# Experts' output rows: two sums by the token's choice, additions without an order, sums read on two queues

## The chip, the core and the metric

The kernel runs on one core of a Trainium2 chip. Its engines are TensorE (PE, matrix products, with PEld for the loading of weights), VectorE (DVE), ScalarE (ACT), GpSimd (POOL) and SyncE (SP). Each works through its own queue of instructions in order; an instruction waits until the semaphores that it names have their values, and everything behind it on that queue waits too. DMAs are issued on SP's, ACT's and POOL's queues and run on 16 DMA engines. The metric is the time of the program on the device in microseconds (us); lower is better.

## What is computed

Four layers over 4096 tokens of 128 numbers: an attention (a, causal), a layer of experts, a second attention (b), and the same layer of experts again, each on the normalised input and added to its input. The layer of experts is what the change is about:

```python
x = x + _L0_attn_a_ref(_layernorm(x, axis=-1), ...)
x = x + _L0_ffn_ref(_layernorm(x, axis=-1), Wr, Wg, Wu, Wd)
x = x + _L0_attn_b_ref(_layernorm(x, axis=-1), ...)
x = x + _L0_ffn_ref(_layernorm(x, axis=-1), Wr, Wg, Wu, Wd)

# _L0_ffn_ref: 8 experts, each token goes to its best two
logits = flat_x @ Wr
top_vals, top_idx = jax.lax.top_k(logits, 2)
rw = jax.nn.softmax(top_vals, axis=-1)
combine = jnp.sum(rw[..., None] * jax.nn.one_hot(top_idx, 8), axis=1)
g = jnp.einsum('nc,ech->neh', flat_x, Wg)      # 128 -> 512
u = jnp.einsum('nc,ech->neh', flat_x, Wu)
h = jax.nn.silu(g) * u
eo = jnp.einsum('neh,ehc->nec', h, Wd) / sqrt(12)
out = jnp.einsum('ne,nec->nc', combine, eo)
```

## The kernel before

**Stages.** `attention` works on 8 blocks (`NB`) of 512 tokens. Its instructions are written out in a fixed order for every engine (the `InOrder` wrappers `te`, `ve`, `se`, `po`, `sy`), by a small planner of tasks with due rounds. At the end of a block, `finish` adds the attention's output to `x`, stores the 512 rows to DRAM (L846) and calls `route`. `route` picks for each token its two experts and writes two copies of its normalised row, one for each choice, to the list of that expert's rows in `rows_in`: 128 numbers, the token's number, and its weight. `both_rows` holds the two copies (index 0 the first choice, 1 the second); the token's number is put in by one copy on GpSimd (L342), from `tokens`, the same number for both.

**Experts.** `experts` then takes the lists in 39 tiles (`TILES`) of 256 rows (`TE`), two halves of 128 (`ET` = 2). For each tile `fetch` loads on SyncE's queue the row block `x_in` (six buffers) and the weights of its expert, `w_g`, `w_u`, `w_d`; `turned` transposes the rows (`xT`); TensorE computes `pg` and `pu`, ScalarE `sg` = silu(`pg`), VectorE `h` = `pu` x `sg`, TensorE `py` from `h` and `w_d`. `finish` of experts multiplies `py` by the rows' weights into `y` (L1015), and for each half of the tile GpSimd issues an indirect DMA that adds 128 rows of `y` to rows of a sum in DRAM (L1019, `compute_op=ALU.add`), at the token numbers in `to`. Outside `attention`, the order of an engine's instructions is chosen when the program is built; program order is only a priority there.

**Where the rows go.** `places` makes `to` in three instructions on VectorE: `here` = 1 for rows of the tile that are filled (L1004), `here` x (token - `nobody`) (L1005), plus `nobody` (L1009). A row that is not filled goes to row 4096 + its partition, which nobody reads. `here` has two buffers, `to` six, `y` four.

**The sums.** For each layer of experts there are two sums, `totals[i][0]` and `totals[i][1]`, DRAM tiles of 4224 rows. The first is filled by the attention's stores (L846), the second with zeros (`zeros`, steps that the first attention spreads over its rounds); the first half of each tile is added to the first, the second half to the second (`sums[(i * ET + s) % 2]`). Since a token's two rows can be added to the same sum, additions to one sum are ordered: each waits until the one before it into the same sum has landed.

**Reading.** The second attention loads a block as `xb` from the first sum and `more` from the second, both on SyncE's queue (L528, L532; `more` has one buffer), and adds them on GpSimd (L541). After the last layer, SyncE's queue loads `a` and `b` for each of 8 blocks, VectorE adds them (L1074) and SyncE's queue stores the result (L1071 to L1075). `tokens_of` gives a partition four rows that lie 128 rows apart, so a DMA moves pieces of one row, 512 bytes.

Instructions issued through an `InOrder` wrapper all show L222 in the profile, whatever line called them; there the names of the tiles tell them apart.

Of the kernel before, what the change touches and what calls it, by code (L numbers as in the profile page):

```python
# [33 lines left out]
F32 = mybir.dt.float32  # L34
# [4 lines left out]
ALU = mybir.AluOpType  # L39
# [3 lines left out]
P = 128  # L43
# [8 lines left out]
NE = 8  # L52
HID = 512
NC = HID // P
TB = 512
NT = TB // P
# [4 lines left out]
ET = TE // P  # L61
CAP = 17 * TE
TOKENS = 4096
W = P + 2
# [6 lines left out]
def layers(  # L71
# [21 lines left out]
    nc = tc.nc  # L93
    xt = x.flatten_outer_dims().rearrange("(n t p) d -> n p t d", t=NT, p=P)
    ot = out.flatten_outer_dims().rearrange("(n t p) d -> n p t d", t=NT, p=P)
    NB = xt.shape[0]
# [17 lines left out]
    def attention_weights(wq, bq, wk, bk, wv, bv, wo, bo, scale, name):  # L114
# [45 lines left out]
    half = const.tile([P, NE], F32, name="half")  # L160
# [14 lines left out]
    tokens = const.tile([P, NB * NT], F32, name="tokens")  # L175
    within = tokens[:, 0:ET]
    nobody = const.tile([P, 1], F32, name="nobody")
# [4 lines left out]
    totals = [  # L182
        [dram.tile([TOKENS + P, P], F32, name=f"total{i}{j}") for j in range(2)] for i in range(2)
    ]
    blank = const.tile([P, 3 * W], F32, name="blank")
    wr_sb = const.tile([P, NE], F32, name="wr_sb")

    def zeros():
# [5 lines left out]
        for first, second in totals:  # L194
            flat = second.rearrange("(p a m) d -> p a (m d)", p=P, m=3)
            for k, m in ((0, 4), (4, 8), (8, 11)):
                to = flat[:, k:m, :]
                yield sy.dma_start(
                    out=to,
                    in_=blank[:, 0 : 3 * P].unsqueeze(1).to_broadcast([P, to.shape[1], 3 * P]),  # L200
                )
            yield sy.dma_start(out=first[TOKENS : TOKENS + P, :], in_=blank[:, 0:P])

# [35 lines left out]
    def later_constants():  # L239
# [19 lines left out]
        for t, pattern, base, by_partition in (  # L259
# [4 lines left out]
            (tokens, [[P, NB * NT]], 0, 1),  # L264
            (nobody, [[0, 1]], TOKENS, 1),
        ):
# [65 lines left out]
    def route(pool, psum, n, xb, free, sent):  # L332
# [11 lines left out]
            tokens[:, n * NT : (n + 1) * NT].unsqueeze(1).to_broadcast([P, 2, NT]),  # L344
# [135 lines left out]
    def tokens_of(total, n):  # L480
        return total[n * TB : (n + 1) * TB, :].rearrange("(t p) d -> p t d", p=P)
# [27 lines left out]
    def attention(w, causal, name):  # L509
        with ExitStack() as own:  # L510
# [11 lines left out]
            def loaded(n):  # L522
# [110 lines left out]
            def scales(n, q, k, junk):  # L633
# [38 lines left out]
                po.tensor_tensor(den, den, half[:, 0:2], ALU.pow)  # L672
# [160 lines left out]
            def finish(n, o):  # L833
# [12 lines left out]
                sy.dma_start(out=tokens_of(totals[0 if causal else 1][0], n), in_=xs[n])  # L846
# [106 lines left out]
    def experts(name, tiles, sums, last):  # L953
        with ExitStack() as own:
# [5 lines left out]
            table, left, sent = tiles  # L960

            def fetch(i):
# [38 lines left out]
            def places(i, x_in):  # L1001

                here = pool.tile([P, ET], F32, tag="here")
                nc.vector.tensor_scalar(here, within, left[:, i : i + 1], None, ALU.is_lt)  # L1004
                nc.vector.scalar_tensor_tensor(  # L1005
                    here, x_in[:, :, P], nobody, here, ALU.subtract, ALU.mult
                )
                to = pool.tile([P, ET], I32, tag="to", bufs=6)
                nc.vector.tensor_scalar(to, here, nobody, None, ALU.add)  # L1009
                return to  # L1010

            def finish(py, i, x_in):
# [5 lines left out]
                for s in range(ET):  # L1018
                    nc.gpsimd.indirect_dma_start(  # L1019
                        out=sums[(i * ET + s) % 2],  # L1020
                        out_offset=bass.IndirectOffsetOnAxis(ap=to[:, s : s + 1], axis=0),
                        in_=y[:, s, :], in_offset=None, compute_op=ALU.add,
                    )

# [91 lines left out]
```

## Time and profile before

| | us |
|---|---|
| three runs | 1331.39, 1349.69, 1356.59 |
| their median | 1349.69 |
| the profiled execution | 1343.86 |
| its span, first to last instruction | 1342.2 |
| stage A, `y` of the first tile to `y` of the 38th | 434.98 to 644.40 |
| second attention's first read of `more` issued | 655.38 |
| stage B, the same | 1098.69 to 1307.54 |
| last addition issued, last store issued | 1314.19, 1338.91 |

The granted TensorE clock was 0.872 of full speed over the span and 1.00 in both stages of experts. Times in the profile are counted from the first instruction. A line of the timeline gives the start, the length, the engine (with q for its sequencer, which issues DMAs), the line, the operation, the tile written and the tiles read, their shape, and in brackets how long the engine was idle before it and what ended that. A wait for several things is put down to the one that came last.

### The profile page before, as it was taken

The page shows a single profiled execution, that of the slowest core. Times are in us where ns is not written, and L with a number is a line of the kernel's source. Part 1 is how long each engine was busy: PE and PEld are TensorE (multiplying, and loading weights), DVE is VectorE, ACT ScalarE, POOL GpSimd, SP SyncE. Part 2 cuts the span into 40 slices and gives each one's busy share as a digit, 9 for nine tenths or more (in the row PEclk, how much of TensorE's full clock was granted, in tenths as well). Part 3 has the DMA queues.
Part 4 walks back from the last instruction along what each step waited for, and adds up shares of the span by engine and source line. Part 5 has one row for each costly group of instructions (what it writes and reads, how often), then busy time and mean ns, then how long its engine had stood idle before and what let it go on. Part 6 is the DMA issues. An engine that isn't in the chain of part 4 may idle for free. (4 is left out here: it accounts for less than half of the span.)

```text
span 1342.2 us, 23350 instructions
## 1 busy us (share of the span) xinstructions
PE 1066.8 (79%) x8116; PEld 771.8 (58%) x8116; DVE 787.6 (59%) x2221; ACT 518.8 (39%) x942; POOL 594.0 (44%) x599
## 2 busy tenths in 40 slices
PE   2799888898763999999457888778877459999990
PEld 1455555555543888888324454445554248888880
DVE  3667667776533555454258787888675535554541
ACT  1156445554521222222135756665555212222220
POOL 7444546655552555555330114233323325555551
PEclk9889878888855999999757999998788779999995
DMA  4244324530015877776253324133300087777757
GB/s 98 51 97 109 72 73 117 138 84 24 25 36 169 210 188 189 180 195 133 45 109 81 66 58 104 51 78 83 89 23 30 27 230 192 178 187 189 189 103 195
DMA packets 175301, 150.84 MB, mean 112 GB/s; under 512 B 14286, under 2 KB 136784, under 8 KB 175184
## 3 DMA queue, kind: packets, MB, share of 16 engines
q1 hardware_dynamic: 145310, 127.18, 34.8%
q0 software_dynamic: 26560, 18.76, 9.4%
q10 hardware_dynamic: 3314, 3.41, 1.1%
q8 instruction: 65, 1.06, 0.3%
q14 instruction: 52, 0.43, 0.1%
HBM read 82.74 MB, written 31.75 MB: 85 GB/s over the span
## 5 line engine op out<-in xcount | busy, mean ns | idle before, releaser
L1019 POOL DMA_INDIRECT total<-y,to x156 | 242.8, 1556 | 229.2 <-DVE here L1005 59.3
L222 DVE TENSOR_REDUCE mx<-s 128x6 f32<-128x768 f32 (+1 forms) x256 | 277.1, 1084 | 110.4 <-PE s L222 109.4
L222 ACT ACTIVATE p<-s 128x768 f32<-128x768 f32 (+1 forms) x256 | 232.9, 916 | 192.2 <-PE s L222 170.2
L1061 ACT ACTIVATE sg<-pg 128x256 f32<-128x256 f32 x312 | 119.4, 383 | 316.8 <-PE pg L1049 300.7
L1063 DVE TENSOR_TENSOR h<-pu,sg 128x256 f32<-128x256 f32 x312 | 131.9, 423 | 149.6 <-PE pu L1053 147.2
L222 POOL DMA_INDIRECT rows_in<-both_rows,slots x128 | 128.9, 1007 | 172.2 <-DVE both_rows L222 113.0
L1053 PE MATMUL pu<-xT,w_u 128*128 128x256 f32 x624 | 190.2, 387 | 5.7 <-DVE h L1063 5.5
L1049 PE MATMUL pg<-xT,w_g 128*128 128x256 f32 x624 | 192.6, 391 | 1.2 <-DMA w_g<-in_L_ffn_Wg_dram 0.7
L1028 PEld LDWEIGHTS py<-w_d,h 128*128 128x128 f32 x1248 | 163.8, 192 | 8.1
L1028 PE MATMUL py<-w_d,h 128*128 128x128 f32 x1248 | 164.6, 275 | 0.0
L222 PE MATMUL s<-k,q 62*128 62x256 f32 (+1 forms) x1024 | 144.3, 367 | 16.1 <-DMA k<-lo 11.4
L222 PE MATMUL s<-q,k 64*128 64x256 f32 (+1 forms) x1024 | 114.2, 307 | 42.1 <-DVE mx L222 33.5
L222 PE MATMUL av<-p,v 128*32 128x256 f32 (+1 forms) x2048 | 144.5, 406 | 0.3 <-ACT au L222 0.2
L222 PEld LDWEIGHTS s<-k,q 62*128 62x128 f32 x1024 | 89.2, 216 | 87.7 <-issue 51.8
L1053 PEld LDWEIGHTS pu<-xT,w_u 128*128 128x128 f32 x624 | 118.0, 192 | 29.6 <-DVE h L1063 13.8
L222 POOL TENSOR_SCALAR_AFFINE_SELECT p<-p 128x512 f32<-128x512 f32 x128 | 82.5, 645 | 108.3 <-ACT p L222 103.7
L222 PEld LDWEIGHTS s<-q,k 64*128 64x128 f32 x1024 | 89.5, 213 | 58.9 <-DVE mx L222 39.7
L1049 PEld LDWEIGHTS pg<-xT,w_g 128*128 128x128 f32 x624 | 102.2, 194 | 20.3 <-issue 13.8
L222 PEld LDWEIGHTS av<-p,v 128*32 128x32 f32 x2048 | 58.7, 120 | 55.2 <-issue 26.4
L222 POOL TENSOR_TENSOR lo<-to,hi 128x512 fp32r<-128x512 f32 x24 | 30.6, 1273 | 72.4 <-ACT hi L222 72.3
L996 PE MATMUL ps<-ident,x_in 128*128 128x128 f32 x156 | 30.6, 279 | 39.1 <-DMA x_in<-rows_in 39.1
L222 PE MATMUL s<-mask_q,ident_h 128*128 128x256 bf16 x256 | 58.6, 317 | 0.0
(206 smaller groups left out, 1179.3 us busy)
## 6 DMA issues: line engine op xcount, KB each, us to landing
w_g<-in_L_ffn_Wg_dram SPq DMA_DIRECT2D x78, 256.0 KB
w_u<-in_L_ffn_Wu_dram SPq DMA_DIRECT2D x78, 256.0 KB
w_d<-in_L_ffn_Wd_dram SPq DMA_DIRECT2D x78, 256.0 KB
x_in<-rows_in SPq DMA_DIRECT2D x78, 130.0 KB
k<-hi SPq DMA_DIRECT2D x32, 256.0 KB
k<-lo SPq DMA_DIRECT2D x32, 256.0 KB
q<-hi SPq DMA_DIRECT2D x28, 256.0 KB
q<-lo SPq DMA_DIRECT2D x28, 256.0 KB
```

Source lines behind the costliest of these rows:

```text
L222: return tc.keep_in_program_order(method(*args, **kwargs))
L996: nc.tensor.transpose(ps[:, bass.ts(s, P)], x_in[:, s, 0:P], ident)
L1019: nc.gpsimd.indirect_dma_start(out=sums[(i * ET + s) % 2], out_offset=bass.IndirectOffsetOnAxis(ap=to[:, s : s + 1], axis=0), in_=y[:, s, ...
L1028: nc.tensor.matmul(py[:, s, :], lhsT=hs[c][:, bass.ts(s, P)], rhs=w_d[:, c, :], start=c == 0, stop=c == NC - 1,)
L1049: nc.tensor.matmul(pg, lhsT=w_g[:, bass.ts(c, P)], rhs=this, start=True, stop=True)
L1053: nc.tensor.matmul(pu, lhsT=w_u[:, bass.ts(c, P)], rhs=this, start=True, stop=True)
L1061: nc.scalar.activation(sg, pg, AF.Silu)
L1063: nc.vector.tensor_tensor(h, pu, sg, ALU.mult)
```

## The change

- The two sums of a layer become one DRAM tile, `totals[i]`, of 2 x 4096 + 8 x 128 rows. `tokens` gets a second plane, 4096 higher, so the second copy of a row carries its token's number + 4096. A first choice is thus added to the first 4096 rows, a second choice to the next 4096, whichever half of a tile it stands in.
- No row then takes more than one addition in a layer, and the additions are declared free of order among themselves (`declare_no_dep`, a group for each layer).
- Rows that are not filled go to one of eight groups of 128 idle rows, by the tile's number (`nobody` has `IDLE` = 8 columns). `places` becomes two instructions: `here` = 0 for filled rows or the idle row's number; `to` = `here` + the number in the row. For this an unfilled row holds the number zero, as before.
- The zeros cover the second 4096 rows and the idle rows, 5120 rows in place of 4224 + 128, in nine steps as before, with pieces of 1024 bytes (1536 before).
- The second attention's first block is read on two queues, `xb` on SyncE's, `more` on ScalarE's (into the buffer of `o`), both after every addition of the layer before (`wait_for`); the other blocks on SyncE's as before.
- The final read takes `a` on SyncE's queue and `b` on ScalarE's, the first of each after every addition; the stores alternate between the two queues; `b` has four buffers. `rows_of` gives a partition four neighbouring rows, so that a DMA moves pieces of 2048 bytes, in the loads and in the stores.

```diff
--- before.py
+++ after.py
@@ -61,6 +61,7 @@
 ET = TE // P
 CAP = 17 * TE
 TOKENS = 4096
+IDLE = 8
 W = P + 2
 TILES = (2 * TOKENS - NE) // TE + NE
 FREE, BUSY, BANK = range(3)
...
@@ -172,17 +172,15 @@
     numbers = const.tile([P, TILES], F32, name="numbers")
     upto = const.tile([P, NE, NE], F32, name="upto")
 
-    tokens = const.tile([P, NB * NT], F32, name="tokens")
-    within = tokens[:, 0:ET]
-    nobody = const.tile([P, 1], F32, name="nobody")
+    tokens = const.tile([P, 2, NB * NT], F32, name="tokens")
+    within = tokens[:, 0, 0:ET]
+    nobody = const.tile([P, IDLE], F32, name="nobody")
 
     chosen = [const.tile([P, NT + 1, NE], BF16, name=f"chosen{i}") for i in range(2)]
     rows_in = dram.tile([(NE + 1) * CAP, W], F32, name="rows_in")
 
-    totals = [
-        [dram.tile([TOKENS + P, P], F32, name=f"total{i}{j}") for j in range(2)] for i in range(2)
-    ]
-    blank = const.tile([P, 3 * W], F32, name="blank")
+    totals = [dram.tile([2 * TOKENS + IDLE * P, P], F32, name=f"total{i}") for i in range(2)]
+    blank = const.tile([P, 3 * P], F32, name="blank")
     wr_sb = const.tile([P, NE], F32, name="wr_sb")
 
     def zeros():
@@ -191,15 +189,14 @@
             out=rows_in[NE * CAP : NE * CAP + TE, :].rearrange("(s p) d -> p s d", p=P),
             in_=blank[:, 0 : ET * W].rearrange("p (s d) -> p s d", s=ET),
         )
-        for first, second in totals:
-            flat = second.rearrange("(p a m) d -> p a (m d)", p=P, m=3)
-            for k, m in ((0, 4), (4, 8), (8, 11)):
+        for total in totals:
+            flat = total[TOKENS:, :].rearrange("(p a m) d -> p a (m d)", p=P, m=2)
+            for k, m in ((0, 5), (5, 10), (10, 15), (15, 20)):
                 to = flat[:, k:m, :]
                 yield sy.dma_start(
                     out=to,
-                    in_=blank[:, 0 : 3 * P].unsqueeze(1).to_broadcast([P, to.shape[1], 3 * P]),
-                )
-            yield sy.dma_start(out=first[TOKENS : TOKENS + P, :], in_=blank[:, 0:P])
+                    in_=blank[:, 0 : 2 * P].unsqueeze(1).to_broadcast([P, to.shape[1], 2 * P]),
+                )
 
     slots = [const.tile([P, 2, NT], I32, name=f"slots{n}") for n in range(NB)]
 
@@ -261,8 +258,8 @@
             (regions, [[CAP, NE]], 0, 0),
             (steps, [[0, NE], [TE, CAP // TE]], 0, 0),
             (numbers, [[1, TILES]], 0, 0),
-            (tokens, [[P, NB * NT]], 0, 1),
-            (nobody, [[0, 1]], TOKENS, 1),
+            (tokens, [[TOKENS, 2], [P, NB * NT]], 0, 1),
+            (nobody, [[P, IDLE]], 2 * TOKENS, 1),
         ):
             po.iota(
                 t, pattern=pattern, base=base, channel_multiplier=by_partition,
@@ -341,7 +338,7 @@
         normed(xn, xb, mv, rstd)
         po.tensor_copy(
             both_rows[:, :, :, P],
-            tokens[:, n * NT : (n + 1) * NT].unsqueeze(1).to_broadcast([P, 2, NT]),
+            tokens[:, :, n * NT : (n + 1) * NT],
         )
         yield 1, BANK
         xnT = turned_block(pool, psum, xn)
@@ -477,8 +474,17 @@
             tc.add_to_no_dep_group(sent[0], pad.ins)
             sent.append(pad)
 
-    def tokens_of(total, n):
-        return total[n * TB : (n + 1) * TB, :].rearrange("(t p) d -> p t d", p=P)
+    def tokens_of(total, i, n):
+        first = i * TOKENS + n * TB
+        return total[first : first + TB, :].rearrange("(t p) d -> p t d", p=P)
+
+    def wait_for(load, scatters):
+        for scatter in scatters:
+            tc.add_manual_dep(
+                load.ins, scatter.ins.name,
+                mybir.DependencyInfo(mybir.DependencyClass.Sync, mybir.DependencyReason.DATA),
+                reason="every row has landed",
+            )
 
     def output_bias(w, pool, psum, name):
 
@@ -506,7 +512,7 @@
         yield 4, BANK
         output_bias(weights_b, pool, psum, "b")
 
-    def attention(w, causal, name):
+    def attention(w, causal, name, landed=()):
         with ExitStack() as own:
             pool = own.enter_context(tc.tile_pool(name=f"att_{name}", bufs=2))
             psum = own.enter_context(tc.tile_pool(name=f"att_{name}_mm", bufs=1, space=PSUM))
@@ -525,11 +531,13 @@
                     xs[n] = x_first
                     return None
                 xb = blocks.tile([P, NT, P], F32, tag="xb")
-                sy.dma_start(out=xb, in_=xt[n] if causal else tokens_of(totals[0][0], n))
+                load = sy.dma_start(out=xb, in_=xt[n] if causal else tokens_of(totals[0], 0, n))
                 xs[n] = xb
                 if not causal:
-                    more = pool.tile([P, NT, P], F32, tag="more", bufs=1)
-                    sy.dma_start(out=more, in_=tokens_of(totals[0][1], n))
+                    more = pool.tile([P, NT, P], F32, tag="more" if n else "o", bufs=1)
+                    second = (sy if n else se).dma_start(out=more, in_=tokens_of(totals[0], 1, n))
+                    for on in (load, second) if n == 0 else ():
+                        wait_for(on, landed)
                     return more
 
             def project(n):
...
@@ -843,7 +851,7 @@
                         ps[:, t, :], lhsT=oT[:, bass.ts(t, P)], rhs=w["wo"], start=True, stop=True
                     )
                 ve.tensor_tensor(xs[n], ps, xs[n], ALU.add)
-                sy.dma_start(out=tokens_of(totals[0 if causal else 1][0], n), in_=xs[n])
+                sy.dma_start(out=tokens_of(totals[0 if causal else 1], 0, n), in_=xs[n])
                 yield 1, BUSY
                 yield from route(pool, psum, n, xs.pop(n), free, sent)
 
@@ -950,7 +958,7 @@
             pads(free[0], sent)
             return *found, sent[1:]
 
-    def experts(name, tiles, sums, last):
+    def experts(name, tiles, total, last):
         with ExitStack() as own:
             pool = own.enter_context(tc.tile_pool(name=f"ffn_{name}", bufs=2))
             psum = own.enter_context(tc.tile_pool(name=f"ffn_{name}_mm", bufs=1, space=PSUM))
@@ -958,6 +966,7 @@
             psum_y = own.enter_context(tc.tile_pool(name=f"ffn_{name}_y", bufs=2, space=PSUM))
 
             table, left, sent = tiles
+            added = []
 
             def fetch(i):
 
@@ -968,14 +977,8 @@
                     out=x_in,
                     in_=rows_in[bass.ds(r, TE), :].rearrange("(s p) d -> p s d", p=P),
                 )
-                for scatter in sent if i == 0 else ():
-                    tc.add_manual_dep(
-                        load.ins, scatter.ins.name,
-                        mybir.DependencyInfo(
-                            mybir.DependencyClass.Sync, mybir.DependencyReason.DATA
-                        ),
-                        reason="every row has landed",
-                    )
+                if i == 0:
+                    wait_for(load, sent)
                 w_g = pool.tile([P, HID], F32, tag="w_g", bufs=4)
                 nc.sync.dma_start(
                     out=w_g, in_=wg[bass.ds(e, 1), :, :].rearrange("o p h -> p (o h)")
@@ -1001,12 +1004,12 @@
             def places(i, x_in):
 
                 here = pool.tile([P, ET], F32, tag="here")
-                nc.vector.tensor_scalar(here, within, left[:, i : i + 1], None, ALU.is_lt)
+                none = nobody[:, i * ET % IDLE : i * ET % IDLE + ET]
                 nc.vector.scalar_tensor_tensor(
-                    here, x_in[:, :, P], nobody, here, ALU.subtract, ALU.mult
+                    here, within, left[:, i : i + 1], none, ALU.is_ge, ALU.mult
                 )
                 to = pool.tile([P, ET], I32, tag="to", bufs=6)
-                nc.vector.tensor_scalar(to, here, nobody, None, ALU.add)
+                nc.vector.tensor_tensor(to, here, x_in[:, :, P], ALU.add)
                 return to
 
             def finish(py, i, x_in):
@@ -1016,11 +1019,15 @@
                     y, py, x_in[:, :, P + 1 : P + 2].to_broadcast([P, ET, P]), ALU.mult
                 )
                 for s in range(ET):
-                    nc.gpsimd.indirect_dma_start(
-                        out=sums[(i * ET + s) % 2],
+                    add = nc.gpsimd.indirect_dma_start(
+                        out=total,
                         out_offset=bass.IndirectOffsetOnAxis(ap=to[:, s : s + 1], axis=0),
                         in_=y[:, s, :], in_offset=None, compute_op=ALU.add,
                     )
+                    group = f"added_{name}"
+                    tc.declare_no_dep(add.ins, group=group, reason="a row takes one addition")
+                    tc.add_to_no_dep_group(group, add.ins)
+                    added.append(add)
 
             def down(s, w_d, hs, py, i, x_in):
 
@@ -1066,17 +1073,24 @@
             for s in range(ET):
                 down(s, *previous)
             if last:
+
+                def rows_of(of, n):
+                    return of.rearrange("(p n m) d -> n p m d", p=P, m=NT)[n]
+
                 for n in range(NB):
                     a = blocks.tile([P, NT, P], F32, tag="xb")
-                    nc.sync.dma_start(out=a, in_=tokens_of(sums[0], n))
-                    b = pool.tile([P, NT, P], F32, tag="b", bufs=3)
-                    nc.sync.dma_start(out=b, in_=tokens_of(sums[1], n))
+                    b = pool.tile([P, NT, P], F32, tag="b", bufs=4)
+                    for i, t, queue in ((0, a, nc.sync), (1, b, nc.scalar)):
+                        load = queue.dma_start(out=t, in_=rows_of(total[i * TOKENS : (i + 1) * TOKENS, :], n))
+                        if n == 0:
+                            wait_for(load, added)
                     nc.vector.tensor_tensor(a, a, b, ALU.add)
-                    nc.sync.dma_start(out=ot[n], in_=a)
+                    (nc.sync, nc.scalar)[n % 2].dma_start(out=rows_of(out.flatten_outer_dims(), n), in_=a)
+            return added
 
     tables = ctx.enter_context(tc.tile_pool(name="tables", bufs=1))
-    experts("a", attention(weights_a, True, "a"), totals[0], False)
-    experts("b", attention(weights_b, False, "b"), totals[1], True)
+    landed = experts("a", attention(weights_a, True, "a"), totals[0], False)
+    experts("b", attention(weights_b, False, "b", landed), totals[1], True)
 
 
 # ---- launch: one core; inputs and outputs as the reference has them ----
```

More of the change, by code (lines that the diff above doesn't have):

```diff
@@ L94, in layers @@
     xt = x.flatten_outer_dims().rearrange("(n t p) d -> n p t d", t=NT, p=P)
-    ot = out.flatten_outer_dims().rearrange("(n t p) d -> n p t d", t=NT, p=P)
     NB = xt.shape[0]
@@ L159, in layers @@
     mask_q = const.tile([P, 2, P], BF16, name="mask_q")
-    half = const.tile([P, NE], F32, name="half")
+    half = const.tile([P, 2], F32, name="half")
     firsts = ident.rearrange("p (j r g) -> p j r g", j=2, r=HD)[:, :, 0, :]
@@ L671, in scales @@
                 ve.tensor_copy(den, ps[:, P : P + 2])
-                po.tensor_tensor(den, den, half[:, 0:2], ALU.pow)
+                po.tensor_tensor(den, den, half, ALU.pow)
                 yield 2, BANK
```

## Prediction

> **What bounds the kernel now.** I read the page first (busy time, slices, chain), then the timeline of the second expert stage engine by engine, the waits of VectorE there, the instructions on the tile `total`, and last the stretch after the last matmul. On the page:
>
> ```profile
> PE 1066.8 (79%) x8116; PEld 771.8 (58%) x8116; DVE 787.6 (59%) x2221; ACT 518.8 (39%) x942; POOL 594.0 (44%) x599
> L1019 POOL DMA_INDIRECT total<-y,to x156 | 242.8, 1556 | 229.2 <-DVE here L1005 59.3
> ```
>
> The two expert stages (39 tiles each) are TensorE's: where nothing disturbs it, one tile follows another in 5.51 us (`y` of two tiles starts at 1098.69 and 1104.20 in the timeline) and PE is busy all of that at clock 1.00. From the first `y` to the last but one are 37 tiles: 435.0 to 644.4 in stage A, 1098.69 to 1307.54 in stage B, so 209.4 and 208.85 us where 37 x 5.508 = 203.8 would do. 5.6 + 5.05 = 10.65 us are lost inside the loops. The rest of the kernel (attention, some 850 us) is touched by the change at one boundary only. Where the 10.65 us go shows in the timeline of VectorE and of GpSimd around one late tile (start, length, instruction, idle time before it and what ended that):
>
> ```profile
> 1126.23 0.42 DVE L1015 TENSOR_TENSOR y<-py,x_in 128x256 f32<-128x256 f32 x1 [0.40 <-PE py L1028]
> 1126.57 0.41 DVE L998 COPY xT<-ps 128x256 f32<-128x256 f32 x1
> 1127.73 0.22 DVE L1005 SCALAR_TENSOR_TENSOR here<-x_in,nobody,here 128x2 f32<-128x2 f32 x1 [0.75 <-DMA x_in<-rows_in]
> 1128.19 0.23 DVE L1009 TENSOR_SCALAR to<-here,nobody 128x2 int32<-128x2 f32 x1 [0.24 <-DMA total<-y,to]
> 1128.33 0.42 DVE L1063 TENSOR_TENSOR h<-pu,sg 128x256 f32<-128x256 f32 x1
> ...
> 1121.58 1.56 POOL L1019 DMA_INDIRECT total<-y,to  x1 [1.75 <-DVE xT L998]
> 1123.44 1.55 POOL L1019 DMA_INDIRECT total<-y,to  x1 [0.30 <-issue]
> 1128.04 1.56 POOL L1019 DMA_INDIRECT total<-y,to  x1 [3.04 <-DVE here L1005]
> ```
>
> `places` of a tile runs six tiles ahead of its addition (its `to` takes the buffer whose additions were issued at 1121.58 and 1123.44), and it stands in VectorE's queue between `xT` and `h`. It waits for two DMAs: L1005 for the row block of that later tile, L1009 for the landing of the additions that used the same `to` buffer. Behind both stands `h`, and TensorE waits for `h`: this tile takes 5.96 us. Three late tiles (L1005 1.50, 1.87 and 1.89 us after `y`; tile late by 0.45, 0.83, 0.82) give the slack: L1005 may start 1.05 us after `y` at no cost. The GpSimd lines show the order between additions: at 1128.04 the first of a pair starts 1.38 us after its `y` is ready (1126.65), because the addition of 1121.58 into the same sum landed only at 1127.3. An undisturbed one starts 0.28 us after its `y` (645.10 against 644.40 + 0.42). The waits of VectorE over stage B (total us, times, longest):
>
> ```profile
> DVE here L1005 <- DMA x_in<-rows_in: 13.3, 18, 3.5
> DVE to L1009 <- DMA total<-y,to: 5.5, 23, 0.5
> ```
>
> Most of L1009's 0.24 us is the step from L1005 to L1009; the row blocks are the longer wait. The tail: after the last addition the sums are read, added and stored on SyncE's queue.
>
> ```profile
> 1314.19 1.55 POOL L1019 DMA_INDIRECT total<-y,to  x1 [0.31 <-issue]
> 1317.58 0.37 SPq L1073 DMA_DIRECT2D b<-total  x1
> 1338.91 0.38 SPq L1075 DMA_DIRECT2D out_dram<-a  x1
> ```
>
> In windows (length, busy of PE, PEld, DVE, ACT, POOL, clock, DMA share, GB/s), a stretch of the loop in which nearly all packets are the 2 KB rows of `w_g`, `w_u`, and the tail with its 512-byte rows:
>
> ```profile
> 1139.00:1141.00 2.00, 2.00 (x14) 1.82 (x13) 1.56 (x5) 0.77 (x2) 1.69 (x2) 1.00 0.68 256
> 1318.00:1338.00 20.00, 0.00 (x0) 0.00 (x0) 4.85 (x7) 0.00 (x0) 0.00 (x0) 0.50 1.00 285
> ```
>
> The tail is 24.6 us (1317.58 to 1342.2) with the 16 DMA engines full: 24 transfers of 256 KB, 6.29 MB, are 22.1 us at 285 GB/s.
>
> **The change part by part.** Base: the profiled execution, 1343.86 us (span 1342.2, 1.7 around it). The median of the three runs, 1349.69, is 5.8 above it.
>
> *Unordered additions, and `places`.* Gone are the waits of an addition for the one before into the same sum. GpSimd's start after `y` becomes 0.28 us for every tile; the second addition follows 1.86 us later (1121.58 to 1123.44) as now, for descriptor making on GpSimd stays (2 x 1.86 = 3.72 us of 5.51). From issue to landing the trace shows 3.2/4.4/6.1 us (least, median, most). VectorE loses one small instruction a tile: `here` needs no row block any more, `to` waits alone for row block and additions. From L1005's start to `h` are now 0.60 us, with `to` alone about 0.15, so the slack grows from 1.05 to 1.5 us after `y`. I went through all tiles with their own landings: keep every latency, start the pair at 0.28 and 2.14 us after `y` is ready, and let the tile be late by what the later of row block and additions lands beyond 1.5 us. That leaves 2.5 us in stage A and 2.2 in B, of the 9.9 that the same tiles show; row blocks alone would leave 1.9 and 1.0. I take **-5.0**, ends 0 (`to` stands as badly as now) and -10.65 (nothing late). What is late next is the row block: it is issued at a fixed place in SyncE's queue, after `w_d`, and lands after up to 4.9 us however the additions are ordered.
>
> *Last additions.* The last four are a chain on GpSimd (1308.43 to 1314.19, 1.86 apart). It can start 0.28 us after 1307.97 instead of 0.46, and the 0.48 us idle before 1312.33 falls to 0.30: **-0.4** at the end; stage A -0.2.
>
> *Final read.* Three things. Rows of 2 KB in place of 512 B: by the two windows a full DMA share moves 256/0.68 = 376 GB/s against 285, so 16.7 us against 22.1, at best -5.4. But that stretch is short, and the mix of the loop moves 187/0.765 = 244 GB/s a full share with additions in it, so zero is the other end; I take 19.0 us, **-3.1**, near the middle, since the better row is the nearer in kind. Next, both first reads now wait for all additions: `a` had a start of one transfer (1315.57) before the last landing, 256 KB or **+0.9**. And the second queue: the DMA engines are already full with one, so it saves no more than an issue (0.5 us) and is taken at **0**; but where out stores block a queue as now (SyncE waits 9.6 us for L1074's adds) a hole could cost up to 2 us. Sum of the tail **-2.2**, ends -5.4 and +2.9.
>
> One rule of the Trainium skill speaks against the larger rows: "DMA: Bandwidth & Descriptors", section Specifications, has line rate from 512 bytes on, so 512-byte rows would lose nothing and the term would be 0, the whole sum 3.1 us smaller. The two windows above disagree with it (285 against 376 GB/s a full share), and I go by them.
>
> *Into the second attention.* Now:
>
> ```profile
> 655.38 0.38 SPq L222 DMA_DIRECT2D more<-total  x1
> 658.39 1.25 POOL L222 TENSOR_TENSOR xb<-xb,more 128x512 f32<-128x512 f32 x1 [5.98 <-DMA more<-total]
> ```
>
> `xb` was issued 3.2 us earlier, so `more` had the engines nearly to itself for the 3.0 us. With one sum for both, `xb` and `more` start together, and the next block's pair follows unblocked: one more transfer ahead of it, 0.26 MB at 285 GB/s = 0.9. Taken **+0.7**, ends -0.2 and +2. ScalarE, which issues `more` and waits for the additions, has nothing behind it but `xnT`, which needs `more` anyway.
>
> *The waits for all additions.* 78 additions on eight semaphores are a few semaphore instructions of 0.02 to 0.05 us on SyncE and on ScalarE, all but the last passed: **+0.1**.
>
> *At nothing:* the constants (a second plane of `tokens`, eight columns of `nobody`) lie in the first attention, where GpSimd is busy half the time; the copy of tokens in `route` has the same size; zeroing goes from 4352 to 5120 rows a sum in as many steps, hidden in the first attention where the DMA share is 0.2 to 0.5. Uncovered it would be 0.8 MB or 2.8 us.
>
> Sum: -5.0 - 0.6 - 2.2 + 0.7 + 0.1 = **-7.0 us**, 1336.9 on the profiled execution, 1342.7 on the median. I say **1340**.
>
> **The rivals.**
> - *All stalls go* (0.12): if the row blocks are late only because of the additions' traffic. For: late row blocks and late additions fall in the same tiles. Against: the additions move the same bytes. -10.65 - 0.6 - 5.4 = -16.7: 1327 (1333 on the median).
> - *The wait moves to the row block and stays* (0.16), or the additions keep an order by some other wait: the loops gain nothing, the rest -2.0: 1342 (1348).
> - *Slower* (0.10): `to` comes to stand ahead of `y` and `xT` in VectorE's queue. Then `h` follows the landing by 0.97 us, and only 0.68 us after `y`'s normal time are free. Row blocks land past that by 0.39 us a tile on average (first 16 tiles of stage A), and with the additions' landings up to 0.6; over 66 tiles +26 to +40 in place of 10.65: net +15 to +29, with the other terms +13 to +27, 1357 to 1371 (1363 to 1377). It decides as soon as `to` is ready in the planned order before `y`; against it, L1005, which has the same need of the row block, stands behind `xT` in all steady tiles.
>
> **How the numbers follow.** My forecast has 0.62. Runs of the kernel before scatter from 1331 to 1357, so a median can sit 10 us off. Range: 1333 less 10 to 1348 plus 5, 1323 to 1353. Two per cent, about what a measurement of this kernel can tell from no change, is 27 us: faster needs 1323 (the first rival with luck): 0.08. Slower needs 1377, the far end of the last: 0.06. The rest, 0.86, is within.
>
> **What would show it.** Additions start 0.28 us after every `y`, the second 1.86 later; the 37 tiles of a stage take 206 to 207 us; `to` still waits, for `x_in`; the tail from last landing to end is 21 to 23 us with the DMA share at 1.0. Wrong if the tile's undisturbed 5.51 us changes, if `to` stands before `y`, or if attention's time moves.

## The result and the profile after

| | before | after |
|---|---|---|
| median of 14 runs each, us | 1348.99 (1331.39 to 1356.59) | 1352.69 (1347.57 to 1357.20) |
| the profiled execution | 1343.86 | 1350.2 |
| its span | 1342.2 | 1348.4 |

The ratio of the compared runs is 1.0103, interval 1.0066 to 1.014: less than two per cent, but not the 7 us gain of the forecast. The comparison leaves out runs of a kernel that lie more than 1.5% above its fastest, which for the kernel before, with a fastest of 1331.39, are five of its 14; without that rule the two medians stand 1.0027 apart, so the medians of all runs are given beside the later ratios. The same kernel on another chip (first experiment below) gave 1.0032, interval 0.999 to 1.0074.

The first thing to do with a span that is 6.2 us longer is to see in which stage it became so. Stages are bounded here by starts of instructions in the timelines: `y` of the first and of the 38th tile of an experts stage, the first and the last maximum `mx` of an attention, and the later of the first reads of `a` and `b`.

| stretch, us | before | after | difference |
|---|---|---|---|
| attention a, first to last `mx` | 324.1 | 324.5 | +0.4 |
| to the first `y` of stage A | 80.64 | 79.94 | -0.7 |
| stage A, 37 tiles | 209.42 | 211.48 | **+2.1** |
| to the first `mx` of attention b | 46.90 | 46.78 | -0.1 |
| attention b, first to last `mx` | 329.04 | 330.93 | +1.9 |
| to the first `y` of stage B | 78.35 | 83.96 | +5.6 |
| stage B, 37 tiles | 208.86 | 209.53 | **+0.7** |
| to the later first read | 10.03 | 9.85 | -0.2 |
| tail, that read to the end | 24.58 | 21.23 | **-3.4** |

The four rows of attention, where the change alters only a copy, the zeroing and the first reads, add up to about +7 us, more than the whole 6.2. The other rows make -0.9: the loops gave back nearly all that the tail gained. So two questions are open: why the loops, forecast at -5.0, came out at +2.7; and whether the attentions' 7 us belong to the change.

The lines that answer to those of before, from the page of the kernel after:

```profile
PE 1066.7 (79%) x8116; PEld 772.5 (57%) x8116; DVE 772.6 (57%) x2143; ACT 518.7 (38%) x942; POOL 594.0 (44%) x599
L1022 POOL DMA_INDIRECT total<-y,to x156 | 242.8, 1556 | 232.7 <-DVE y L1018 165.0
```

VectorE has 78 instructions and 15 us less work, and GpSimd's additions now wait for `y` and no more for one another, as meant. A late tile in VectorE's timeline, stage A (start, length, instruction, idle time before it and what ended that):

```profile
474.21 0.42 DVE L1018 TENSOR_TENSOR y<-py,x_in 128x256 f32<-128x256 f32 x1 [0.40 <-PE py L1035]
474.55 0.42 DVE L1001 COPY xT<-ps 128x256 f32<-128x256 f32 x1
476.89 0.16 DVE L1012 TENSOR_TENSOR to<-here,x_in 128x2 int32<-128x2 f32 x1 [1.92 <-DMA total<-y,to]
477.09 0.22 DVE L1008 SCALAR_TENSOR_TENSOR here<-tokens,left,nobody 128x2 f32<-128x2 f32 x1
477.23 0.75 DVE L1070 TENSOR_TENSOR h<-pu,sg 128x256 f32<-128x256 f32 x2
...
481.08 0.42 DVE L1018 TENSOR_TENSOR y<-py,x_in 128x256 f32<-128x256 f32 x1 [0.40 <-PE py L1035]
```

`to` here belongs to a tile five ahead. It starts 2.68 us after `y`, `h` follows 0.34 us later, and the next `y` comes after 6.87 us in place of 5.51. Two things are to be seen. The wait is ended by an addition, not by the row block. And `here`, 0.22 us, now stands between `to` and `h`; before, nothing stood between L1009 and `h`. The waits of VectorE over stage A say the same of all tiles (total us, times, longest):

```profile
DVE to L1012 <- DMA total<-y,to: 19.9, 23, 1.9
DVE to L1012 <- DMA x_in<-rows_in: 0.5, 1, 0.5
```

In stage B it is 17.9 us in 25 waits for additions. GpSimd at the last four additions, and the tail in a window (length, busy of PE, PEld, DVE, ACT, POOL, clock, DMA share, GB/s):

```profile
1318.20 1.56 POOL L1022 DMA_INDIRECT total<-y,to  x1 [2.27 <-DVE y L1018]
1320.06 1.56 POOL L1022 DMA_INDIRECT total<-y,to  x1 [0.30 <-issue]
1321.92 1.56 POOL L1022 DMA_INDIRECT total<-y,to  x1 [0.30 <-issue]
1323.78 1.55 POOL L1022 DMA_INDIRECT total<-y,to  x1 [0.30 <-issue]
```

```profile
1329.00:1347.00 18.00, 0.00 (x0) 0.00 (x0) 5.52 (x8) 0.00 (x0) 0.00 (x0) 0.50 0.93 338
```

The chain of the last additions has lost its one hole, and the tail moves 338 GB/s where it moved 285.

### The profile page after: what moved, and what is told of

The parts are those of the page before. It is cut to its first block, busy times and chain, and to the rows that moved or that the text cites. A ratio compares the mean times of both kernels' runs of the same rounds, so it can differ in the third digit from the quotient of the medians.

```text
span 1348.4 us, 23285 instructions
## 1 busy us (share of the span) xinstructions
PE 1066.7 (79%) x8116; PEld 772.5 (57%) x8116; DVE 772.6 (57%) x2143; ACT 518.7 (38%) x942; POOL 594.0 (44%) x599
```

## The experiments

In what follows the floor of a loop is 37 undisturbed tiles, 37 x 5.51 = 203.8 us. Theory: the loops lose their time where `to` stands in VectorE's queue. It is placed five tiles ahead of its own addition, with six buffers, so it takes the buffer of the tile whose additions were issued one tile (5.5 us) ago, and it waits for their landing in front of `h`. Rivals: the loss is in the row blocks; the additions without an order disturb the loads; attention has become slower through the change.

**The kernel after, once more.** No edit.

> The changed kernel once more, against the kernel before on one chip. Theory (the change moves only the expert stages and the tail): by the two profiles the loops' 37 tiles go from 209.4 + 208.9 to 211.5 + 209.5 us, the tail from the last landing to the end from 24.6 to 21.3, the step into the second attention stays: sum about -1 us, so a ratio of 0.995 to 1.005, and loops of 209 to 212 us again. Rival (the attention is slowed by the change): ratio 1.007 to 1.014 again, with the loops as before.

It took 1358.27 us, the kernel before beside it 1356.80, ratio 1.0032 (0.999 to 1.0074), and in its profile the loops took 215.5 and 211.3 us, stage A more than the 209 to 212 expected and than any reading before. The tail was 20.9. A loop that waits for landings differs from execution to execution by several us, so a difference of 2 or 3 us between two single profiles says little about it.

**`to` later, in the kernel after.** One added dependence: `to` of tile i comes after `y` of tile i-2, so it can be at most two tiles ahead, and the buffer it takes was used four tiles ago.

```diff
-                nc.vector.tensor_tensor(to, here, x_in[:, :, P], ALU.add)
+                filled = nc.vector.tensor_tensor(to, here, x_in[:, :, P], ALU.add)
+                if i > 1:
+                    tc.add_manual_dep(filled.ins, products[i - 2].ins.name, ...)
```

> The changed kernel, but `to` of a tile is held back until `y` of the tile two before it, so it stands two tiles ahead and not five, and neither its buffer nor its row block is still awaited. Theory (what is lost in the loops is `to` in front of `h` in VectorE's queue, waiting for the additions that used its buffer): 37 tiles take 203.8 to 204.5 us in both stages, 12 us less than the changed kernel. Rival (the unordered additions load the DMA engines so that weights or row blocks come late, or GpSimd holds VectorE up): the loops stay at 208 us or more, with PE waiting for something else.

Both loops took the floor, 203.77 and 203.78 us, and the ratio is 0.9837 (0.9769 to 0.9905); the medians of all runs are 1340.96 and 1356.80. VectorE's timeline in stage A and its longest waits in stage B (there is no line for `to` any more):

```profile
473.99 0.42 DVE L1025 TENSOR_TENSOR y<-py,x_in 128x256 f32<-128x256 f32 x1 [0.40 <-PE py L1043]
474.33 0.41 DVE L1002 COPY xT<-ps 128x256 f32<-128x256 f32 x1
474.66 0.22 DVE L1013 TENSOR_TENSOR to<-here,x_in 128x2 int32<-128x2 f32 x1
474.92 0.22 DVE L1009 SCALAR_TENSOR_TENSOR here<-tokens,left,nobody 128x2 f32<-128x2 f32 x1
475.14 0.42 DVE L1078 TENSOR_TENSOR h<-pu,sg 128x256 f32<-128x256 f32 x1
```

```profile
DVE h L1078 <- PE pu L1068: 77.7, 98, 1.3
DVE y L1025 <- PE py L1043: 16.5, 39, 1.5
DVE h L1078 <- PE pg L1064: 4.3, 8, 0.8
DVE h L1078 <- ACT sg L1076: 2.0, 4, 0.5
DVE h L1078 <- issue: 1.8, 4, 0.5
```

The five instructions stand in the same sequence as after the change, with no idle time in them. The place is the same; only the tile that `to` belongs to is another. Nearly every wait is for TensorE, and none for a DMA. Landing takes no less time than in the profile after the change (5.0 and 4.4 us against 4.9 and 4.2, medians of the first and second addition of a pair): no transfer became faster.

**Twelve buffers for `to`.** This takes away the wait for additions and leaves `to` five tiles ahead.

```diff
-                to = pool.tile([P, ET], I32, tag="to", bufs=6)
+                to = pool.tile([P, ET], I32, tag="to", bufs=12)
```

> The changed kernel with twelve buffers of `to` in place of six: the order on VectorE stays, `to` then waits only for its row block. Theory: stalls fall to those of late row blocks, 37 tiles in 204.5 to 207.5 us. If row blocks were as bad as additions (what the prediction said is late next), 209 us or more stay.

The loops took 207.9 and 208.9 us, more than the 204.5 to 207.5 expected, ratio 0.9945 (0.991 to 0.998), medians 1349.15 and 1356.80. VectorE's waits in stage B:

```profile
DVE h L1070 <- PE pu L1060: 73.9, 95, 1.3
DVE to L1012 <- DMA x_in<-rows_in: 17.6, 24, 2.4
```

Now the row block is the wait, and a larger one than the forecast left for it (4.1 and 5.1 us of lateness, not 1.9 and 1.0). Two DMAs stand behind one place in the queue; to remove one shows the other. Of these edits only the later place removes both.

**The same lateness in the kernel before.** The dependence of the second experiment, put on L1005, with two ordered sums and everything else as before.

```diff
-                nc.vector.scalar_tensor_tensor(
+                filled = nc.vector.scalar_tensor_tensor(
                     here, x_in[:, :, P], nobody, here, ALU.subtract, ALU.mult
                 )
+                if i > 1:
+                    tc.add_manual_dep(filled.ins, products[i - 2].ins.name, ...)
```

> The kernel before, ordered additions and all, with `places` held back until `y` of the tile two before. Theory (the order between additions costs only through VectorE's wait): 37 tiles take 203.8 to 205 us although additions still wait for one another, about 10 us less than before; the unordering by itself is then worth nothing in the loops. Rival (the ordered additions are a chain nearly as long as a tile, 4.4 + 0.7 us against 5.5, and pile up until `y` waits for its buffer): 206 to 209 us.

203.77 and 203.76 us, ratio 0.987 (0.9809 to 0.9931), medians of all runs 1344.08 and 1356.80. VectorE's waits in stage B begin

```profile
DVE h L1071 <- PE pu L1061: 76.0, 103, 1.7
DVE y L1022 <- PE py L1036: 15.4, 36, 1.5
```

and name neither `here` nor `to`. So the order between the additions costs the loops nothing by itself: a first addition starts on average 1.1 us after its `y` here and the loop is at its floor all the same. All of the 10.65 us of before, and all of what the kernel after loses, is the place of `places`.

**The kernel before, against itself.** No edit. What two sets of runs of one program differ by is the measure for the ratios above.

> The kernel before against itself: how far a ratio lies from 1 with nothing changed, and what its loops are on this chip. Theory (a few tenths of a per cent in the total are the attention's throttled clock and say nothing of the change): ratio anywhere from 0.995 to 1.005, attention times several us apart from the first profile of the same kernel, loops of 37 tiles near 209 us each. Rival: ratio within 0.002 of 1 and equal attention times; then the changed kernel's 1.01 needs a cause in the attention.

The ratio is 0.9979 (0.9942 to 1.0017), medians 1347.38 and 1348.78. The loops took 210.2 and 211.7 us, so before's own scatter between executions reaches 2.9 us in a stage, as much as the differences that I wanted to read. And its span was 1330.1 us, 12 less than the profile of before, with slower loops. Attention a of the two executions, in windows of the same work (matmul counts agree within the few records that miss; columns as above, the clock third from the end); first before as shown, then here:

```profile
30.30:354.00 323.70, 281.61 (x2537) 175.29 (x2541) 219.08 (x532) 150.56 (x224) 170.94 (x220) 0.86 0.33 81
```

```profile
30.30:336.60 306.30, 261.23 (x2542) 164.76 (x2545) 219.57 (x534) 150.13 (x224) 171.09 (x220) 0.93 0.35 86
```

The same 220 instructions of GpSimd take 171 us in both; PE's take 282 at a granted clock of 0.86 and 261 at 0.93, and the stage is by these windows 17.4 us shorter.

**The kernel after a third time**, beside the run above.

> The changed kernel a third time, on the chip of e5, for the loops alone: theory (the loops are slower with the change, 211.5 and 209.5 against 209.4 and 208.9 in the first pair) 210 to 216 us each and more than those of e5. Rival (no difference beyond the scatter between profiles): within 1 us of e5.

1355.81 us in its one run; loops 213.8 and 211.8, tail 21.1, attention a 324.4 at a clock of 0.853. Only stage A is slower than in the kernel before on the same chip (210.2 and 211.7); stage B is level with it.

**`here` made once**, ahead of the loop for all tiles; nothing then stands between `to` and `h`.

```diff
+            heres = pool.tile([P, TILES, ET], F32, tag="heres", bufs=1)
+            nc.vector.tensor_tensor(heres, within..., left..., ALU.is_ge)
+            ...
-                here = pool.tile([P, ET], F32, tag="here")
-                nc.vector.scalar_tensor_tensor(here, within, left[:, i : i + 1], none, ...)
+                here = heres[:, i, :]
```

> The changed kernel with `here` of all tiles made once ahead of the loop, so that `to` alone stands before `h`. Theory (`here` stands before `h` too and takes 0.2 us off the slack, 1.31 us after `y` in place of the 1.5 that the prediction had): each loop about 2 us shorter than in e6, 206 to 211 us. Rival (only the landings of the additions count): within 0.5 us of e6.

Loops 209.6 and 208.4, against 211.5 to 215.5 and 209.5 to 211.8 in the three profiles with `here` in the loop. VectorE's timeline, a late tile of stage A:

```profile
456.75 0.16 DVE L1020 TENSOR_TENSOR to<-heres,x_in 128x2 int32<-128x2 f32 x1 [1.84 <-DMA total<-y,to]
456.86 0.76 DVE L1078 TENSOR_TENSOR h<-pu,sg 128x256 f32<-128x256 f32 x2
```

From `to` to `h` are 0.11 us, not 0.34: 0.23 us of slack are back. The slack can be read off each late tile, as the start of `to` after `y` less the lateness of the tile. In tiles late by more than 0.3 us it is 1.32 us in nearly all of the three profiles with `here` in the loop, 1.52 in nearly all of the two profiles of the kernel before, and 1.54 in every one here. The total of its one run, 1324.56, is 24 us below before's median beside it, but its attention a took 306.7 us at a clock of 0.94; it is not a measure of `here`.

**Rows of 512 bytes again, two queues kept.**

```diff
-                    return of.rearrange("(p n m) d -> n p m d", p=P, m=NT)[n]
+                    return of.rearrange("(n m p) d -> n p m d", p=P, m=NT)[n]
```

> The changed kernel with the final read in rows of 512 bytes again, on the two queues. The tail from the issue of the last first read to the end was 24.6 us before and 21.2 with the change. Theory (the larger rows are the gain, the DMA engines being full with one queue already): 24 to 25.5 us. Rival (the second queue is the gain): 21 to 22 us.

The tail took 23.5 us, against 20.9 to 21.2 with rows of 2 KB; that lies between the two expectations. Its window:

```profile
1322.00:1340.00 18.00, 0.00 (x0) 0.00 (x0) 5.54 (x8) 0.00 (x0) 0.00 (x0) 0.50 1.11 306
```

306 GB/s to 338 with the larger rows. A DMA share of 1.11 can't be a part of a whole; from here on only the rates are read.

**Rows of 2 KB kept, one queue again.**

```diff
-                    for i, t, queue in ((0, a, nc.sync), (1, b, nc.scalar)):
+                    for i, t, queue in ((0, a, nc.sync), (1, b, nc.sync)):
...
-                    (nc.sync, nc.scalar)[n % 2].dma_start(out=rows_of(out.flatten_outer_dims(), n), in_=a)
+                    nc.sync.dma_start(out=rows_of(out.flatten_outer_dims(), n), in_=a)
```

> The changed kernel with the final read and the stores all on SyncE's queue, rows of 2048 bytes kept. The tail (last first read to the end) was 24.6 and 25.4 us in two profiles of the kernel before, 20.9 to 21.2 with the change, 23.5 with rows of 512 bytes on two queues. Theory (the rows give most, the second queue the rest): 21.5 to 23.5 us. Rival (the second queue gives nothing, the engines being full): 20.9 to 21.3. Rival (it gives most): 24 or more.

27.6 us: within "24 or more", the case that the second queue gives most, but also more than the 24.6 of before with small rows, which no expectation had. SyncE's queue in the timeline, and the window:

```profile
1334.78 0.34 SPq L1088 DMA_DIRECT2D out_dram<-a  x1
1335.16 0.43 SPq L1084 DMA_DIRECT2D a<-total  x1
1338.60 0.34 SPq L1088 DMA_DIRECT2D out_dram<-a  x1
1338.99 0.43 SPq L1084 DMA_DIRECT2D b<-total  x1
...
1341.10 0.38 SPq L1084 DMA_DIRECT2D a<-total  x1
1344.71 0.34 SPq L1088 DMA_DIRECT2D out_dram<-a  x1
1345.10 0.42 SPq L1084 DMA_DIRECT2D b<-total  x1
```

```profile
1332.00:1356.00 24.00, 0.00 (x0) 0.00 (x0) 5.54 (x8) 0.00 (x0) 0.00 (x0) 0.50 0.76 244
```

Between 1335.6 and 1338.6, and between 1341.5 and 1344.7, nothing is issued: a store waits for its sum, and the next `b` stands behind it, which the sum after that needs. The rate falls to 244 GB/s. In all, SyncE waits 14.4 us for the sums here and 9.6 in the kernel before. Why the holes on one queue are longer with large rows than with small ones stays open.

One sentence of the Trainium skill ("DMA: Bandwidth & Descriptors", section "Issuing engines are not separate DMA queues") says that issuing from several engines only saves the sequencer's time for the issue, which is usually small. The measurement here differs: 27.6 to 21.1 us for 24 issues, because what a second queue saves is also the wait of reads behind a store that isn't ready.

**The new tail in the kernel before**: larger rows, two queues and four buffers of `b`, with two ordered sums.

> The kernel before with the new final read alone (rows of 2048 bytes, two queues, four buffers of b; the sums as before). Theory (the parts do not depend on one another): tail 20.5 to 21.5 us, loops 209 to 212 us each as before. Rival (the tail gains because both sums end together): tail over 22.5 us.

The loops took 211.3 and 209.7 us, as before. The tail took 21.24 us and 10.57 from the 38th `y` to the later first read: 31.8, where the kernel after took 31.1, 30.8 and 31.0 in its three profiles. The tail's gain needs no unordered additions.

**Both in the kernel before**: that tail, and `places` later.

> The kernel before with `places` held back (e4) and the new final read (e10): ordered additions, split by the half of the tile. Theory (the order of the additions costs nothing once nothing on VectorE waits for them): as fast as e12, loops 203.8 us, ratio 0.980 to 0.990, within 0.004 of e12. Rival (freedom of order is worth something by itself): e12 faster by 3 us or more in loops, step and last additions.

Loops 203.75 and 203.75, tail 20.6, 1342.91 us (1322.9 to 1344.12) beside 1354.27 of the kernel before, ratio 0.9871 (0.9795 to 0.9946).

**`to` later in the kernel after, once more**, beside the last two.

> The changed kernel with `to` held back, once more beside e11. Theory: loops 203.8 us, ratio 0.980 to 0.990. If the first ratio of 0.984 was the attention's scatter alone, it falls to 0.995 or more.

Loops 203.75 and 203.75, tail 20.9, ratio 0.982 (0.9741 to 0.9898). By the medians of all runs it is 12 us below the kernel before (1342.61 and 1354.27), in the second experiment 16. The segments show 14 to 19 (loops and end: 438.2 and 439.0 us, before 452.9 and 457.4).

The kernel before with both edits is level with it: a median of 1342.91, loops and end 438.5 us, and an interval that overlaps. Loops, step and last additions differ by 1.1 us in all, not by the 3 of the rival. So the two sums by choice and the freedom of order, the idea of the change, are worth no more than about 1 us here; the place of `places` and the new final read give the gain without them.

## Why the prediction was wrong, and where it was right

The kernel before and the kernel after, in what the change touches, from two profiles of before and three of after (means, us; the two loops at their floor took 407.5):

| | before | after | difference | forecast |
|---|---|---|---|---|
| both loops | 420.1 | 424.5 | +4.4 (first pair +2.7) | -5.0 |
| last additions and waits for them, to the first read | 10.1 | 9.9 | -0.2 | -0.3 |
| step into attention b | 47.0 | 46.9 | -0.1 | +0.5 |
| tail | 25.0 | 21.1 | -3.9 (first pair -3.4) | -2.2 |
| sum | | | **+0.2** | **-7.0** |

With the runs that alter only the final read, the two loops took 418.3, 421.0 and 421.9 us as in the kernel before, and 421.0, 424.0, 425.6, 426.0 and 426.8 as in the kernel after: slower by some 4 us on the mean, though the ranges meet. The median of 1352.7 does lie within the stated 1323 to 1353, at its end; that is no support for the forecast, as the range was that wide for the scatter of runs, and the term that carried the forecast had the wrong sign.

**The loops, the step that failed.** The forecast said "with `to` alone about 0.15, so the slack grows from 1.05 to 1.5 us after `y`", "keep every latency", and "What is late next is the row block". Each of the three was wrong.

- *The slack.* 1.05 was L1005's, and 1.5 was already the slack of the instruction that waits for the additions, L1009: in the forecast's own late tile it started 1.96 us after `y` for a lateness of 0.45. The wait for additions thus gained nothing from the shorter `places`. It lost: `here` came to stand behind `to`. I had taken it to lie elsewhere in the queue, as L1004 did. In the kernel after, the late tile above gives 2.68 - 1.36 = 1.32, and so do nearly all others. With `here` made once the loops are shorter by 1.2 to 5.9 us than in any of the three profiles with it.
- *The latencies.* First additions start 0.28 us after `y`, as forecast, against a mean of 0.73 before. But they take longer to land: medians of 4.9 and 4.2 us (first and second of a pair) against 4.7 and 4.0, and 5.0 and 5.1 for the first in the repeats. A pair started 0.45 us sooner has landed 6.9 us after its `y` started in place of 7.0, on average, and 7.0 again in the repeats: 0.1 us won, or nothing. In the other direction, starts 1.1 us after `y` land in 4.5 and 3.5.
- *What is late next.* The additions of the tile before, still. They land on average 6.9 - 5.51 = 1.4 us after the `y` that follows, and `to` must start by 1.32. Before it was 7.0 - 5.51 = 1.5, and 1.52 was allowed. So the typical tile stood at the edge before and stands just past it now, and the spread of landings decides each tile. The forecast had 2.5 and 2.2 us late in the two stages; measured are 7.7 and 5.7, and 7.5 to 11.7 in the repeats.

The deeper error is that both stalls were treated as amounts to be saved when both came from one choice: a small instruction for a tile five ahead, in VectorE's queue in front of work for this tile. The forecast even has the words "`places` of a tile runs six tiles ahead" (by the timeline it is five; the buffer's last additions lie six tiles behind), and draws no consequence from it. Undone, it gives all that the loops lose over their floor, 10.7 and 14.4 us in the two profiles of the kernel before, 13.5 to 19.3 in the three of the kernel after; the unordered additions give none of it, as the fourth experiment shows.

**The tail: right in sign, by luck in its largest term.** Transfers: 6.29 MB at 338 GB/s are 18.6 us, and the forecast had 19.0. But it had them for the larger rows alone, with the second queue at 0. On one queue the larger rows move 244 GB/s and the tail is 27.6 us, longer than the 24.6 and 25.4 of before; on two queues they shorten it by 2.3 to 2.7 us, from 23.5. The second queue is worth 2 us or less with small rows (23.5 against 24.6 and 25.4, where buffers and waits differ too) and 6.5 with large ones. So the two parts can't be added up one by one. The forecast named the hole behind a store, up to 2 us, as a chance and let "the DMA engines are already full" decide; with the larger rows on one queue the holes are 3 us each, and they are the limit. The lost head start of `a` (+0.9) did not appear: with the new tail in the kernel before, where the first `a` is read 2.4 us ahead of `b`, the end took 31.8 and 31.0 us, and in the kernel after 30.8 to 31.1.

**The step into attention b** costs nothing: 46.78 to 47.08 us in three profiles, 46.90 and 47.09 before. The term of +0.7 for one more transfer ahead did not show; -0.2 of the additions may hide as much.

**The rivals.** The one that the wait "stays" was nearest, though the wait went from the row block to the additions and not the other way. Its form with the wait at the row block is the kernel with twelve buffers. *All stalls go* came about only through the later place, with additions and loads as they were. The one with `to` ahead of `y` did not come about: `to` follows `xT` in all steady tiles.

**Attention.** Is its time changed by the change? All four stretches of attention add up to 812.1 and 795.2 us in the two profiles of before and to 819.3, 818.0 and 820.2 in the three of after. But the variants share the scatter: those made from before show 826 to 828, those made from after 797 to 833. The mean over five profiles with before's attention code is 817.7 and over nine with after's 818.1. So no effect of the change is seen. Not settled is the 1.0103 itself: none of the 27 runs of the kernel after came below 1344.5 us, while two of the first 14 of before took 1331 and 1332. Runs as fast as that come where attention a has the higher clock (before: 306 us at 0.93), and two kernels made from the kernel after had it (306.7 and 308.4 us). That points to chance, but a true slowdown between 0 and 1% is not excluded by it; in the sum of the stages that the change touches it isn't there.

## What to carry to other kernels

When a small instruction waits for a DMA in an in-order queue, ask first which tile it belongs to: one that is planned too far ahead takes a buffer that was used too short a time ago, and removing the order, a buffer or one of its waits only brings out the next; placing it later brought all of it at once. Before a shorter latency is counted as a gain, check which instruction's slack it meets, and what the planner puts into the place that came free. Where two stretches of one profile differ by less than the same stretch between two executions of one kernel (here 3 to 4 us in a loop, 17 in an attention), take the difference from an experiment that removes the cause, not from the pair.

## What the runs showed of the hardware

- An indirect addition started sooner takes longer to land while weights are being loaded: mean start 0.28, 0.73 and 1.1 us after `y`, median landing 4.9, 4.7 and 4.5 us after issue. With starts 0.45 us sooner the first of a pair landed some 0.2 us sooner, and the whole pair 0.1 us sooner or not at all. In the last two tiles of a stage of the kernel after, where no loads are left, it is 3.2 to 3.3. That the loads' packets are what it queues behind is an inference; no run took the loads away.
- With larger rows on one queue the final read took 27.6 us (one profile), against 24.6 and 25.4 with rows of 512 bytes in the kernel before, which also has other waits and one buffer of `b` fewer; on two queues it took 21.1 against 23.5, with the rows alone changed.
- Attention a has a granted clock near 0.855 in some executions of a program and near 0.93 in others, 322 to 325 us against 306 to 308 (two executions with 317 us had 0.849). One execution that differs in this moves the total by 17 us, about as much as the later `to` does.
